# A complex MLP between two FFTs: one gelu over two PSUM banks, and eight PSUM banks split into four single and two double

## The chip, the core and the metric

The kernel runs on one core of a Trainium2 chip. A core has a matrix engine (TensorE, PE in the profile) that writes only to PSUM, three engines that read it or the on-chip memory SBUF (VectorE = DVE, ScalarE = ACT, GpSimd = POOL; POOL does not touch PSUM here), and queues for DMA. PSUM has eight banks; one bank holds 512 float32 values on each of 128 partitions. Each engine works through its own instructions in a fixed order and waits on semaphores for the others. The metric is device time in microseconds of one execution, lower is better.

## What is computed

The input is 8 images of 192 channels and 64 x 64 pixels, float32. Two layers follow each other. In short:

```python
# layer 0: attention in 8x8 windows over the 16 best keys, then an MLP
xs  = layernorm(x)                       # over channels
att = l2n(q) @ l2n(k).T * temperature
att = where(att >= kth_largest_16, att, -100) + rpb
x2  = xs + proj(softmax(att) @ v)
x2  = x2 + gelu(layernorm(x2) @ fc1) @ fc2
# layer 1: a small complex MLP between a 2D FFT and its inverse, then an MLP
freq = stack([real, imag](fft2(layernorm(x))))   # 2 values a frequency
h    = gelu(freq @ fc1.T + b1) @ fc2.T + b2      # 2 -> 16 -> 2, for each frequency
x    = x + ifft2(complex(h)).real
out  = x + gelu(layernorm(x) @ mlp1) @ mlp2
```

## The kernel before

One image at a time is held as `y` (channels on partitions). Layer 0 (`layer0`, `attention`, `mlp`) goes over 8 bands of 8 rows; each band has two halves of four attention windows. Layer 1 (`layer1`) first transposes the image so that rows lie on partitions (`px`, L411), then handles 24 blocks of 4 + 4 channels, transposes back (`pr`, L519) and ends with an MLP by bands.

One of the 24 blocks is a chain: normalization on POOL (L440, L444), a first DFT product `fa` (L454), copy on DVE (L462), a second DFT product `fz` (L464), copy (L466), then the pointwise complex MLP in two halves `hf`, then `fo` with its bias to SBUF (L491), and the inverse DFT products `fb` (L494) and `fy` (L508), each copied by DVE (L502, L511).

A half of the complex MLP has four first products `fh` (L472). They use 32 rows of the array each ("row tiles" k = 0..3) and each fills one bank. Four gelus on ACT (L481) bring these to SBUF, one bank each. Four second products (L482) each take one gelu output and use 32 columns of the array ("column tiles"); all write into the same bank `fo`, at 32 partitions each. The profile counts two matmul records for each float32 product, so a half has 8 records of L472 and 8 of L482.

All PSUM tiles come from one pool of eight one-bank buffers. A tile takes a free buffer and gives it back after its last reader. `fo` is held over both halves. The MLP (`mlp`, L196 to L214) holds two accumulators `mo` and takes a bank `mh` for each of six steps: first product L196, gelu L204 to the SBUF tag `h`, second product L206.

The parts of layer 0 and layer 1 are generators. While layer 0 of one image is issued, layer 1 of the image before is issued between its steps: 112 steps of layer 0 to 144 of layer 1, by a counter. A block of the FFT part has four such steps: normalization; `fa`, `fz` and the first half; the second half; `fo` to `fy`. The order within each engine follows this source order, except where an instruction's forerunners had not been placed yet when the engine's turn came; then a later one steps in. Layer 1 of the last image runs alone.

Of the kernel before, what the change touches and what calls it, by code (L numbers as in the profile page):

```python
# [8 lines left out]
FP = mybir.dt.float32  # L9
# [5 lines left out]
C = 192  # channels  # L15
HC = 96  # channels of one partition chunk
HW = 64  # rows, columns of an image; also tokens of one attention window
BAND = 512  # tokens of one band of 8 rows
# [6 lines left out]
def kernel(  # L25
# [6 lines left out]
    """Layer 0: layernorm, 8x8-window attention over the 16 best keys, projection, MLP.  # L32
    Layer 1: layernorm, FFT2, a pointwise complex MLP, inverse FFT2, MLP.

    One image at a time: `y` [96, 2, 4096] keeps its channels on partitions (channel
    c = 96 * chunk + partition) from layer 0's projection to the result. The FFTs are
    matrix products with 64-point DFT matrices, which take the data as the stationary
    operand where an axis has to change to the partitions.
    """
# [8 lines left out]
        tc.tile_pool(name="psp", bufs=8, space=bass.MemoryType.PSUM)  # L48
# [16 lines left out]
    vecs = load("vecs", [HC, 16])  # per-channel vectors, the two chunks of each side by side  # L65
    (g1, b1, g2, b2, fc2b, n2g, n2b, mlp2b) = (vecs[:, 2 * i : 2 * i + 2] for i in range(8))
    n1 = const.tile([128, 2, HC], FP, tag="n1", name="n1")  # on the partitions of each chunk
# [6 lines left out]
    # the biases of these two are a 193rd row, which the ones in row 96 of xn and ot multiply  # L74
# [8 lines left out]
    # relative position bias: partition (c, query), free (h3, key), head 3 c + h3. It is read  # L83
    # with the keys in reverse, where all of the table's strides are positive.
# [18 lines left out]
    # DFT matrices: two 64-point ones on the diagonal (fcos, fsin), and complex ones  # L103
    halves = load("halves", [128, 128])  # averages the two chunks' partitions
# [5 lines left out]
    # the pointwise complex MLP. Frequencies v lie on partitions as (v // 16, re/im, v % 16);  # L110
    # hidden values of 8 of them as (hidden 16, v % 8).
# [21 lines left out]
    # layer 0's normalized bands and heads' outputs, window by window, with a row of ones  # L133
# [8 lines left out]
    def windows(band):  # L142
        """A band's tokens [p, 512], as [p, row, window, column]."""
        return band.rearrange("p (r w k) -> p r w k", r=8, w=8)

    def layernorm(src, gam, bet, dst, nm, by_window=False):
        """src, dst [96, 2, 512]; by_window: dst's tokens are in the order of windows."""
# [42 lines left out]
    def mlp(hn, w1, bias1, w2, bias2, res, nm):  # L190
        """res [96, 2, 512] += gelu(hn @ w1 + bias1) @ w2 + bias2"""
        acc = [psum(f"mo_{nm}_{c}") for c in range(2)]
        for f in range(6):
# [9 lines left out]
            h = sb.tile([128, BAND], FP, tag="h", name=f"h_{nm}_{f}", bufs=5)  # L203
# [14 lines left out]
    # The parts below are generators: they yield between steps, so that one image's layer 1  # L218
    # can be issued between the steps of the next image's layer 0.

    def attention(xn, hb, nm):
        """Windows 4 hb .. 4 hb + 3 of a band: xn -> heads' outputs in ot."""
# [16 lines left out]
        # q and k by their norms, q by the temperature  # L239
# [32 lines left out]
        # scores: partition (c, query), free (h3, window, key)  # L272
# [18 lines left out]
        # where(s >= the 16th largest, s, -100) + rpb  # L291
# [22 lines left out]
        # softmax  # L314
# [14 lines left out]
        # keys to the partitions: (window of a pair, key), free (h3, pair, c, query)  # L329
# [23 lines left out]
        # a window's place is 4 hb + 2 p + w2  # L353
        ow = ot[:HC, :, 256 * hb : 256 * hb + 256].rearrange("q c (p w t) -> q w c p t", p=2, w=2)
        for w2 in range(2):
            nc.vector.tensor_copy(
                ow[:, w2], po[w2][:HC, :256].rearrange("q (c p t) -> q c p t", c=2, p=2)
            )

    def layer0(b, y):  # L360
        """x[b] -> y, by bands of 8 rows"""
        for i in range(NB):
            nm = f"{b}_{i}"
            yb = y[:, :, i * BAND : (i + 1) * BAND]
# [271 lines left out]
```

## Time and profile before

Three runs took 12977.23, 12985.01 and 12985.38 us, median 12985.01. All further numbers are of one profiled execution.

| | before |
|---|---|
| median of the runs | 12985.01 us |
| the profiled execution, span from first to last instruction | 12957.8 us (27.2 us under the median; nothing around it is listed) |
| PE busy | 8896.2 us, 69% |
| DVE / ACT / POOL busy | 3575.0 / 2861.4 / 1881.7 us |
| mean granted TensorE clock | 0.755 of full speed |
| complex MLP: first products, gelus, second products, busy | 820.7 / 945.1 / 1320.2 us |

In the profile, "L482 PE MATMUL fo<-fh,w2t x8" means eight records of the matmul on line 482, which write the tile `fo` from `fh` and `w2t`. A number in square brackets is the idle time of that engine just before, with the engine and line that ended it. Busy times of overlapping matmuls are modelled, so starts are firmer than ends. A granted clock of 0.5 means that the matrix engine got half of its clock pulses.

### The profile page before, as it was taken

How to read it: one execution, taken by the hardware profiler on the slowest of the kernel's cores; microseconds unless marked ns; L12 is line 12 of the kernel's file. 1: busy time of each engine (PE TensorE's matmuls, PEld its weight loads, DVE VectorE, ACT ScalarE, POOL GpSimd, SP SyncE). 2: the span in 40 equal slices, each digit the busy share in tenths (PEclk: the TensorE clock that was granted, in tenths of full speed). 3: DMA queues.
4: the chain of work that ended last, by engine and by line, in shares of the span. 5: the costliest groups of instructions: out<-in, count | busy, mean ns of one | idle time of the engine just before them, and what ended most of it. 6: DMA issues, size and time to landing. Idle time of an engine off the chain costs nothing.

```text
span 12957.8 us, 100088 instructions
## 1 busy us (share of the span) xinstructions
PE 8896.2 (69%) x38816; PEld 3927.9 (30%) x38816; DVE 3575.0 (28%) x12526; ACT 2861.4 (22%) x4820; POOL 1881.7 (15%) x1874
## 2 busy tenths in 40 slices
PE   4455776857768577685776766767667676767778
PEld 2222323323333233332333322333223332333323
DVE  2323223222232322323223222232222322232211
ACT  1111222212221222212222122221222212222121
POOL 1113011130011301103101131011211103011200
PEclk7666777867778677786777867778677776777898
DMA  0000000000000000000000000000000000000000
GB/s 17 3 4 3 3 2 3 10 4 3 3 3 9 4 3 3 3 11 2 3 3 3 11 2 3 3 4 10 3 2 3 5 9 3 2 3 3 8 1 10
DMA packets 28818, 60.28 MB, mean 5 GB/s; under 512 B 6834, under 2 KB 9331, under 8 KB 28340
## 3 DMA queue, kind: packets, MB, share of 16 engines
q1 hardware_dynamic: 21172, 28.70, 0.8%
q0 software_dynamic: 7168, 25.17, 0.7%
q8 instruction: 304, 4.98, 0.2%
q14 instruction: 174, 1.43, 0.0%
HBM read 28.69 MB, written 25.17 MB: 4 GB/s over the span
## 4 chain that ended last, share of the span: by engine, by line
PE 61%; DVE 18%; POOL 14%; ACT 5%; issue 2%; SPq 0%; DMA 0%; POOLq 0%; ACTq 0%; DVEq 0%
PE mo_l L206 12%; PE mh_l L196 12%; PE fo L482 8%; PE fh L472 5%; POOL nrm L251 4%; PE pq L233 3%; PE pp L380 2%; DVE s L298 2%; PE qt L264 2%; PE fy L508 2%; POOL xy L440 2%; PE fz L464 2%; PE fa L454 2%; PE fb L494 2%; POOL s L307 2%
## 5 line engine op out<-in xcount | busy, mean ns | idle before, releaser
L482 PE MATMUL fo<-fh,w2t 128*32 128x512 f32 x3072 | 1320.2, 791 | 254.6 <-ACT fh L481 254.6
L481 ACT ACTIVATE fh<-fh,ab 128x512 f32<-128x512 f32 x1536 | 945.1, 691 | 1738.1 <-PE fh L472 1732.1
L264 PE MATMUL qt<-ident,qk 128*96 128x128 f32 x1024 | 248.6, 424 | 1272.1 <-DVE qk L256 1272.1
L204 ACT ACTIVATE h_l<-mh_l,fcb 128x512 f32<-128x512 f32 x768 | 527.9, 687 | 2522.5 <-PE mh_l L196 2519.3
L472 PE MATMUL fh<-fz,w1t 32*128 32x512 f32 x3072 | 820.7, 879 | 205.6 <-DVE fz L466 205.6
L196 PE MATMUL mh_l<-hm,wmlp 96*128 96x512 f32 x1536 | 867.4, 694 | 30.1 <-ACT hm L182 30.1
L206 PE MATMUL mo_l<-h_l,wmlp 128*96 128x512 f32 x1536 | 846.3, 680 | 56.8 <-ACT h_l L204 56.8
L206 PE MATMUL mo_l<-h_l,wfc 128*96 128x512 f32 x1536 | 790.3, 639 | 57.3 <-ACT h_l L204 56.9
L196 PE MATMUL mh_l<-hn,wfc 96*128 96x512 f32 x1536 | 798.1, 643 | 9.8 <-ACT hn L182 9.8
L482 PEld LDWEIGHTS fo<-fh,w2t 128*32 128x32 f32 x3072 | 224.7, 121 | 1269.7 <-ACT fh L481 1117.6
L214 DVE SCALAR_TENSOR_TENSOR y<-mo_l,vecs,y 96x512 f32<-96x512 f32 x256 | 190.5, 746 | 1512.9 <-PE mo_l L206 1499.5
L264 PEld LDWEIGHTS qt<-ident,qk 128*96 128x96 f32 x1024 | 186.2, 196 | 1319.0 <-DVE qk L256 1311.3
L307 POOL TENSOR_TENSOR s<-s,rpb 128x768 f32<-128x768 f32 x128 | 231.1, 1805 | 2249.5 <-DVE mask L302 2087.6
L464 PE MATMUL fz<-fa,fwd 128*128 128x512 f32 x384 | 307.4, 893 | 364.0 <-DVE fa L462 364.0
L233 PE MATMUL pq<-wqkv,xn 96*128 96x384 f32 (+1 forms) x1024 | 527.4, 602 | 16.2 <-ACT xn L182 16.2
L251 POOL TENSOR_TENSOR nrm<-nrm,mhalf 128x24 f32<-128x24 f32 x128 | 536.9, 4194 | 10.1
L241 POOL TENSOR_TENSOR sq<-qk 128x768 f32<-128x768 f32 x128 | 187.8, 1467 | 2175.7 <-ACT qk L236 2175.7
L196 PEld LDWEIGHTS mh_l<-hm,wmlp 96*128 96x128 f32 x1536 | 338.8, 226 | 474.8 <-issue 407.4
L269 ACT COPY qkt<-qt 96x512 f32<-96x512 f32 x256 | 149.4, 584 | 1398.4 <-PE qt L264 1398.4
L491 DVE TENSOR_SCALAR fo<-fo,ab 128x512 f32<-128x512 f32 x192 | 143.4, 747 | 1109.7 <-PE fo L482 1109.7
L196 PEld LDWEIGHTS mh_l<-hn,wfc 96*128 96x128 f32 x1536 | 316.8, 210 | 433.7 <-issue 407.2
L334 PE MATMUL at<-ident,a 128*128 128x128 f32 x768 | 167.2, 366 | 392.6 <-DVE a L324 392.6
(120 smaller groups left out, 12085.9 us busy)
## 6 DMA issues: line engine op xcount, KB each, us to landing
xin<-in_x SPq DMA_DIRECT2D x64, 384.0 KB
out<-y POOLq DMA_DIRECT2D x64, 384.0 KB, 3.4
wfc<-in_wfc SPq DMA_DIRECT2D x2, 576.0 KB
wmlp<-in_wmlp SPq DMA_DIRECT2D x2, 576.0 KB
rrev<-in_rpb SPq DMA_DIRECT2D x48, 2.0 KB
wqkv<-in_wqkv SPq DMA_DIRECT2D x1, 218.2 KB
wqkv<-in_wqkv SPq DMA_DIRECT2D x1, 216.0 KB
n<-in_n SPq DMA_DIRECT2D x2, 48.0 KB
```

Of the source, the lines that this page charges most:

```text
L196: nc.tensor.matmul(ph, w1[:, c, f * 128 : (f + 1) * 128], hn[:, c, :], start=(c == 0), stop=(c == 1),)
L204: nc.scalar.activation(h, ph, AF.Gelu, bias=bias1[:, f : f + 1])
L206: nc.tensor.matmul(acc[c][:HC, :], w2[:, f, c * HC : (c + 1) * HC], h, start=(f == 0), stop=(f == 5),)
L233: nc.tensor.matmul(dst, tok, wqkv[:k, c, cols], start=(c == 0), stop=(c == 1))
L251: nc.gpsimd.tensor_tensor(nf, nf, mhalf[:, :24], ALU.pow)
L264: nc.tensor.transpose(pt[:HC, c * 256 + p * 128 : c * 256 + (p + 1) * 128], qk[:, p, j * C + c * HC : j * C + (c + 1) * HC], ident,)
L298: nc.vector.match_replace(s2[:, h3, wi], top[:, i, 0], s[:, h3, wi], -3.0e38)
L307: nc.gpsimd.tensor_tensor(s, s, rpb.unsqueeze(2).to_broadcast([128, 3, 4, 64]), ALU.add)
L464: nc.tensor.matmul(pz, fwd2, fa, start=True, stop=True)
L472: nc.tensor.matmul(phs[k], w1t[rows, hf].rearrange("p h v -> p (h v)"), fz[rows, :], start=True, stop=True,)
L481: nc.scalar.activation(h, phs[k], AF.Gelu, bias=ab[:, 0:1])
L482: nc.tensor.matmul(po[32 * k : 32 * k + 32, :], w2t[:, hf].rearrange("p a v -> p (a v)"), h, start=(hf == 0), stop=(hf == 1),)
```

## The change

The four one-bank tiles of a half become two tiles of two banks (`psum_wide`, from a pool of its own with two buffers). One gelu covers both banks of such a tile, 1024 columns. Its output `fh` has its own SBUF tag with three buffers of 1024 columns. The second products are issued in a loop of their own after both gelus. The one-bank pool shrinks from eight buffers to four, which now serve everything else. The tag `h` goes from five to three buffers (only the MLPs use it now), the tag `f` from four to three. Comments and docstrings are dropped; lines after the pool are some numbers further down in the new file.

```diff
     psp = ctx.enter_context(
-        tc.tile_pool(name="psp", bufs=8, space=bass.MemoryType.PSUM)
+        tc.tile_pool(name="psp", bufs=4, space=bass.MemoryType.PSUM)
+    )
+    psw = ctx.enter_context(
+        tc.tile_pool(name="psw", bufs=2, space=bass.MemoryType.PSUM)
     )
...
+    def psum_wide(name):
+
+        return psw.tile([128, 2, 512], FP, tag="pw", name=name)
...
-            h = sb.tile([128, BAND], FP, tag="h", name=f"h_{nm}_{f}", bufs=5)
+            h = sb.tile([128, BAND], FP, tag="h", name=f"h_{nm}_{f}", bufs=3)
...
-            f32 = lambda name: sb.tile([128, 512], FP, tag="f", name=f"{name}_{nm}", bufs=4)
+            f32 = lambda name: sb.tile([128, 512], FP, tag="f", name=f"{name}_{nm}", bufs=3)
...
             for hf in range(2):
-                phs = [psum(f"fh_{nm}_{hf}_{k}") for k in range(4)]
+
+                phs = [psum_wide(f"fh_{nm}_{hf}_{j}") for j in range(2)]
                 for k in range(4):
                     rows = slice(32 * k, 32 * k + 32)
                     nc.tensor.matmul(
-                        phs[k],
+                        phs[k // 2][:, k % 2],
                         w1t[rows, hf].rearrange("p h v -> p (h v)"),
                         fz[rows, :],
                         start=True,
                         stop=True,
                     )
+                hs = []
+                for j in range(2):
+                    h = sb.tile([128, 2, 512], FP, tag="fh", name=f"fh_{nm}_{hf}_{j}", bufs=3)
+                    nc.scalar.activation(h, phs[j], AF.Gelu, bias=ab[:, 0:1])
+                    hs.append(h)
                 for k in range(4):
-                    h = sb.tile([128, 512], FP, tag="h", name=f"fh_{nm}_{hf}_{k}", bufs=5)
-                    nc.scalar.activation(h, phs[k], AF.Gelu, bias=ab[:, 0:1])
                     nc.tensor.matmul(
                         po[32 * k : 32 * k + 32, :],
                         w2t[:, hf].rearrange("p a v -> p (a v)"),
-                        h,
+                        hs[k // 2][:, k % 2],
                         start=(hf == 0),
                         stop=(hf == 1),
                     )
```

## The prediction

> **What bounds the kernel now.** I read the page first, for which engine carries the chain that ended last and which groups of the complex MLP cost most.
>
> ```profile
> span 12957.8 us, 100088 instructions
> ...
> PE 61%; DVE 18%; POOL 14%; ACT 5%; issue 2%; SPq 0%; DMA 0%; POOLq 0%; ACTq 0%; DVEq 0%
> ...
> L482 PE MATMUL fo<-fh,w2t 128*32 128x512 f32 x3072 | 1320.2, 791 | 254.6 <-ACT fh L481 254.6
> L481 ACT ACTIVATE fh<-fh,ab 128x512 f32<-128x512 f32 x1536 | 945.1, 691 | 1738.1 <-PE fh L472 1732.1
> ...
> L472 PE MATMUL fh<-fz,w1t 32*128 32x512 f32 x3072 | 820.7, 879 | 205.6 <-DVE fz L466 205.6
> ```
>
> PE, in the order in which it was given its work, is the chain for 61% of the span; ACT as an engine is far from full, but its gelus stand inside PE's waits. So what counts is how long PE needs from the first `fh` of a block to its last `fo`. There are 192 blocks (8 images x 24), 384 halves.
>
> Then the timeline of the last image's FFT part, where nothing else runs: one half undisturbed.
>
> ```profile
> 12343.51 1.14 PE L472 MATMUL fh<-fz,w1t 32*128 32x512 f32 x8
> 12344.73 2.42 ACT L481 ACTIVATE fh<-fh,ab 128x512 f32<-128x512 f32 x4 [2.25 <-PE fh L472]
> ...
> 12345.47 2.78 PE L482 MATMUL fo<-fh,w2t 128*32 128x512 f32 x8 [0.82 <-ACT fh L481]
> ...
> 12348.29 0.75 DVE L491 TENSOR_SCALAR fo<-fo,ab 128x512 f32<-128x512 f32 x1 [9.50 <-PE fo L482]
> ```
>
> Four row-tiled products take 1.14 us together, then four gelus in 2.42 us set the pace, and the last second product ends 1.05 us after the last gelu. 4.74 us in all. The column-tiled products already overlap: each starts when its gelu is done, 0.58 us apart.
>
> Third, the timeline over all 192 blocks, for PE's order within each. Counted by that order there are six patterns: 38 blocks straight (first products, second products, twice), 42 with the scores `s` between the halves, 21 with a whole attention projection step, 21 with a whole layer-0 MLP between the halves, 35 with `at` transposes among the second products of the first half, and 35 of this kind (matmuls first, then ACT):
>
> ```profile
> 6292.75 2.09 PE L472 MATMUL fh<-fz,w1t 32*128 32x512 f32 x8 [2.35 <-DVE fz L466]
> 6295.60 1.91 PE L482 MATMUL fo<-fh,w2t 128*32 128x512 f32 x2 [0.76 <-ACT fh L481]
> 6297.45 2.08 PE L472 MATMUL fh<-fz,w1t 32*128 32x512 f32 x4
> 6299.76 1.91 PE L482 MATMUL fo<-fh,w2t 128*32 128x512 f32 x2 [0.23 <-ACT fh L481]
> 6301.60 2.07 PE L472 MATMUL fh<-fz,w1t 32*128 32x512 f32 x2
> 6303.60 1.92 PE L482 MATMUL fo<-fh,w2t 128*32 128x512 f32 x2
> 6305.45 2.07 PE L472 MATMUL fh<-fz,w1t 32*128 32x512 f32 x2
> 6307.45 3.62 PE L482 MATMUL fo<-fh,w2t 128*32 128x512 f32 x10
> ```
> ```profile
> 6294.86 0.69 ACT L481 ACTIVATE fh<-fh,ab 128x512 f32<-128x512 f32 x1 [11.46 <-PE fh L472]
> 6295.57 1.28 ACT L321 ACT_TABLE_LOAD   x1
> 6296.86 0.84 ACT L321 ACTIVATE a<-a 128x768 f32<-128x768 f32 x1
> ...
> 6299.02 3.00 ACT L481 ACTIVATE fh<-fh,ab 128x512 f32<-128x512 f32 x5
> ```
>
> The softmax's exp, with its table load and the one back to gelu, stands in ACT's order between the first gelu and the second. PE's order was made round it: one second product, then first products of the other half, one at a time. A row-tiled and a column-tiled product don't run together: each change costs about 2 us, as much as four of a kind side by side. These blocks take 18.35 us from the first `fh` to L491; a straight one with its clock at half (6.55 us a half, from 6226.09 to 6232.64) would take some 12.5 to 13.
>
> ```profile
> 6292.70:6311.10 18.40, 17.32 (x32) 3.06 (x32) 3.96 (x5) 8.47 (x11) 0.00 (x0) 0.50 0.00 0
> ```
>
> In this row of the view by windows (length, then PE, weight loads, DVE, ACT and POOL busy, then the granted clock) PE is busy for 17.32 us and yet has half its clock throughout.
>
> **The change, part by part.**
>
> *Wide gelus in order.* A copy on ACT of 256 columns takes 380 ns (L288), of 512 columns 584 ns (L269): 0.80 ns a column. So a second bank adds 0.41 us, and a wide gelu takes 0.69 + 0.41 = 1.10 us; a second one ends 0.58 + 0.41 = 0.99 later. Two wide gelus: 2.09 us against 2.42, a gain of 0.33 a half. The first second product waits 0.41 longer, which costs nothing, since the last gelu sets the end; the last two then run side by side in 1.05, as the overlapping pairs do now. Of 384 halves, 70 lie in the 35 blocks with exp, 42 second halves (after `s`) end behind DVE's search for the largest keys, where L491 waits anyway, and 21 second halves follow the MLP and are taken there. 251 x 0.33 = 83 us gain. Ends: 50 (more of them end in DVE or POOL waits) and 115 (all).
>
> *Blocks with exp.* After the first wide gelu two second products are free, not one, and of the other half only the first pair of first products finds a wide buffer. PE's order should be 4 fh, 2 fo, 2 fh, 2 fo, 2 fh, 4 fo. With half-clock rows: 2.09 + 0.02 + 1.10, then exp's 3.47 (from the end of a gelu to the next, 6295.55 to 6299.02), second gelu ends at 7.8; two second products to 9.7, two first ones to 11.8, last gelu to 12.9, two second ones to 14.9. Gain 18.35 - 14.95 = 3.4. If exp goes ahead of both or behind both, halves stay whole: 2.09 + 3.47 + 2.1 + 2.0 + 2.09 + 2.1 + 2.0, with the waits between 16.1, gain 2.2. Taken: between the two, 2.85 x 35 = 100 us. Ends: 0 (a new alternation as long as the old) and 6 x 35 = 210 (straight).
>
> *Four banks for all else, the layer-0 MLP.* I counted from the timeline, for each one-bank tile other than `fh`, how many other such tiles are live when its first product starts, and how long until only three are. 166 us of waiting in all, not overlapped. Its largest part is this place:
>
> ```profile
> 6176.81 1.96 PE L206 MATMUL mo_l<-h_l,wfc 128*96 128x512 f32 x4
> 6178.60 1.88 PE L196 MATMUL mh_l<-hn,wfc 96*128 96x512 f32 x4
> ...
> 6186.87 1.12 PE L472 MATMUL fh<-fz,w1t 32*128 32x512 f32 x2
> ```
>
> In 21 MLPs (three an image, seven images) `fo` is held from the first half to the second. With `fo` and two `mo` live, one bank is left for `mh`. Today PE starts the next `mh` before the gelu of the last is read; with one bank it waits: 84 times, 0.95 us each, 80 us. What is queued behind is everything PE does later. What covers it is the first products of the second half, which have buffers of their own and already slip in once (row 6186.87). If one slips into each of four gaps (1.05 each, one gap of 0.83 left) then the three products and four gelus that now follow the MLP (4.1 us to the end of `fo`, 6189.81 to 6193.97) shrink to 1.1: net cost 1 us an MLP, 20 in all. Taken 60, nearer to the counted row. Ends 20 and 88 (5 gaps x 0.83 x 21).
>
> *Four banks, elsewhere.* The rest of the count is 87 us: scores or `at` that start while a layer-1 MLP still holds two `mo` and an `mh` (46 us), transposes `px` beside `s` (10), layernorm tiles, `pr`. A part repeats the same wait for tiles queued behind each other, `px` is a filler. Taken 40; ends 10 and 87. Layer-1 MLPs never meet `fo`, so two `mh` remain, and PE is one `mh` ahead at most: nothing.
>
> *At nothing:* gelu outputs three deep and `h` three deep (PE is never more than two steps behind a gelu); `f` three deep (`fb` takes the place of `fa`, whose reader is two products back); copies of layer 0 behind a wide gelu wait up to 0.41 us more, beside PE's first products. No DMA moves.
>
> *Sum:* -83 - 100 + 60 + 40 = -83 us: span 12875. The profiled execution's 12957.8 is 27 under the median of 12985.0, so 12902.
>
> The Trainium skill ("TensorE: Matmul & The Clock Gate", Part 1) says that about 3.4 us of sustained activity bring the full clock; the row above, 17 us busy at half clock, disagrees, as if a quarter of the array did not count as activity. By the page the new order in these 35 blocks would run at full clock and end with ACT at some 10 us, an estimate of -290 for that term in place of -100.
>
> **The rivals.**
> *A, the alternation stays.* PE's order is laid down anew and exp may fall where first and second products still take turns. For it: the pattern comes from the order of placing, which durations shift. Against: only two turns are possible. Then -83 + 60 + 40 = +17: 13002.
> *B, slower: one bank too few.* PE takes everything in order, so a wait for a bank also delays what stands behind it, and that its own bank. If the 166 us of waits pass on a second time, the cost is 332, the sum +149, 13134; at 1.25 times, 13010. It decides from 183 us of cost. Against: `fh` leaves this pool, and more than four other tiles are live for only 148 us of the span.
> *C, the clock.* With longer gaps before `fo` more halves run at half clock: 6.55 against 4.74 us, 1.8 each. From 46 of 384 halves on, the gain is gone; at 80, 12902 + 144 = 13046. Against: the last image keeps 1.00 with gaps of 1.75 us.
> *D, better.* The 35 blocks go straight (-210) and fillers hide the bank waits (30 for both): -263, 12722.
>
> **How the numbers follow.** Forecast 0.46, its own range 12830 to 12960; A 0.18, B 0.14, C 0.06, D 0.16. To leave out 2 in 10, the range goes to 12740 (most of D) and to 13040 (A, and the smaller prices of B). 0.2% is 26 us, about what a measurement of this kernel can tell from none. Faster: forecast (0.44 of it) and D, 0.61 with a little of A; same: most of A's middle, 0.13; slower: the upper part of A, B, C, 0.26.
>
> **What would show it.** Gelus: 768 records of about 1.10 us; straight halves of 4.4 us. Blocks with exp: order 4-2-2-2-2-4 at about 15 us. MLPs with `fo` held: single `fh` records between `mh` and `mo`, or PE idle of 0.8 before `mo` on gelu L204. Wrong if PE's order shows other alternations, if `s` or `mh` wait for banks by more than 100 us, or if the granted clock falls below 0.73.

## The result, and the profile after

The changed kernel takes 13138.53 us (median of four runs, 13120.13 to 13151.71), the kernel before 12985.19 beside it: a ratio of 1.012, with a 95% interval from 1.0105 to 1.0134. It is slower, where 12902 was forecast with a range of 12740 to 13040. Its profiled execution has a span of 13118.4 us against 12957.8, and a mean granted clock of 0.746 against 0.755. The two spans lie 20 and 27 us under their medians; stages and blocks below are read from such single executions.

The page of the kernel after: span, the chain of waits by engine, and the groups of second products, gelus and first products (busy, mean of one in ns, then the idle time before them).

```profile
span 13118.4 us, 98779 instructions
...
PE 60%; DVE 18%; POOL 13%; ACT 6%; issue 2%; SPq 0%; DMA 0%; POOLq 0%; ACTq 0%; DVEq 0%
...
L493 PE MATMUL fo<-fh,w2t 128*32 128x512 f32 x3072 | 1069.3, 831 | 561.0 <-ACT fh L490 561.0
L490 ACT ACTIVATE fh<-fh,ab 128x1024 f32<-128x1024 f32 x768 | 817.1, 1113 | 1531.7 <-PE fh L480 1531.3
...
L480 PE MATMUL fh<-fz,w1t 32*128 32x512 f32 x3072 | 834.2, 862 | 203.5 <-DVE fz L473 203.5
```

The wide gelu costs what was worked out, 1.11 us, and ACT's busy time for these gelus falls by 128 us (945.1 to 817.1). But PE's wait in front of the second products more than doubles, from 254.6 to 561.0 us.

The timeline of the last image, where nothing else runs, one block. Each row has its start, its length, the engine and the operation.

```profile
12567.55 1.14 PE L480 MATMUL fh<-fz,w1t 32*128 32x512 f32 x8 [0.78 <-DVE fz L473]
12568.78 2.12 ACT L490 ACTIVATE fh<-fh,ab 128x1024 f32<-128x1024 f32 x2 [11.34 <-PE fh L480]
12569.95 1.05 PE L493 MATMUL fo<-fh,w2t 128*32 128x512 f32 x4 [1.26 <-ACT fh L490]
12570.93 1.12 PE L480 MATMUL fh<-fz,w1t 32*128 32x512 f32 x2
12571.98 1.85 PE L493 MATMUL fo<-fh,w2t 128*32 128x512 f32 x4
12573.76 1.98 PE L480 MATMUL fh<-fz,w1t 32*128 32x512 f32 x6
12575.83 2.12 ACT L490 ACTIVATE fh<-fh,ab 128x1024 f32<-128x1024 f32 x2 [4.93 <-PE fh L480]
12577.00 2.06 PE L493 MATMUL fo<-fh,w2t 128*32 128x512 f32 x8 [1.26 <-ACT fh L490]
```

Two records are one product here. PE waits 1.26 us for a wide gelu where it waited 0.82 for a narrow one. And a block that was straight (four first, four second products, twice) is now 4-2-1-2-3-4: one first product of the other half stands between the two pairs of second products. The next pair of second products takes 1.85 us where the first took 1.05: the clock has dropped in between.

The view by windows over 100 us of the last image (length, then busy time of PE, weight loads, DVE, ACT and POOL, the granted clock, the DMA share and GB/s), first the kernel before, then the kernel after:

```profile
12350.00:12450.00 100.00, 71.79 (x367) 26.21 (x365) 18.76 (x29) 29.07 (x48) 0.00 (x0) 1.00 0.00 1
```
```profile
12500.00:12600.00 100.00, 72.56 (x302) 25.64 (x302) 15.16 (x24) 21.20 (x20) 0.00 (x0) 0.83 0.00 0
```

PE is just as busy and finishes 302 matmul records in place of 367: its mean clock has fallen from 1.00 to 0.83.

A block with exp, matmuls and ACT in order of time:

```profile
6321.98 2.09 PE L480 MATMUL fh<-fz,w1t 32*128 32x512 f32 x8 [2.29 <-DVE fz L473]
...
6323.85 1.28 ACT L328 ACT_TABLE_LOAD   x1 [11.23 <-DVE a L325]
6325.15 0.84 ACT L328 ACTIVATE a<-a 128x768 f32<-128x768 f32 x1
...
6327.30 2.12 ACT L490 ACTIVATE fh<-fh,ab 128x1024 f32<-128x1024 f32 x2
6328.47 1.92 PE L493 MATMUL fo<-fh,w2t 128*32 128x512 f32 x4 [4.40 <-ACT fh L490]
6330.32 2.07 PE L480 MATMUL fh<-fz,w1t 32*128 32x512 f32 x2
6332.32 1.92 PE L493 MATMUL fo<-fh,w2t 128*32 128x512 f32 x4
6334.18 2.00 PE L480 MATMUL fh<-fz,w1t 32*128 32x512 f32 x6
```

The exp now stands ahead of both gelus, PE waits 4.40 us for it, the products on both sides of the wait run at half clock (2.09 and 1.92 us), and then first and second products still take turns, though fewer times than before.

Two tables show where the time went. The first cuts the profiled span at the first and last matmul of each stage: sums over images 0 to 6, and then the last image's FFT part.

| us | before | after | change |
|---|---|---|---|
| first image's layer 0 | 1057.5 | 1064.2 | +6.7 |
| FFT parts, images 0 to 6 | 6951.6 | 6947.2 | -4.4 |
| `pr`, images 0 to 6 | 794.4 | 808.2 | +13.8 |
| layer-1 MLPs, images 0 to 6 | 2232.5 | 2276.9 | +44.4 |
| last image's FFT part | 417.1 | 522.9 | +105.8 |
| all else | 1504.7 | 1499.0 | -5.7 |

The second gives the mean time of a block, from its first `fh` to the bias that takes its `fo`, by what stands among its products. It is taken from the timeline of each kernel. PE idle inside it is in brackets.

| blocks | number | before | after | sum of the change |
|---|---|---|---|---|
| exp | 35 | 18.39 (1.07) | 17.85 (5.65) | -19 |
| scores `s` | 42 | 13.06 (2.63) | 13.53 (3.36) | +20 |
| `at` transposes | 35 | 13.66 (0.76) | 14.58 (2.52) | +32 |
| layer-0 MLP | 21 | 34.16 (1.67) | 33.96 (1.26) | -4 |
| attention projection | 21 | 34.04 (18.01) | 30.91 (16.59) | -66 |
| others, images 0 to 6 | 14 | 9.47 (1.66) | 11.36 (3.08) | +26 |
| last image | 24 | 9.63 (1.67) | 12.44 (2.58) | +67 |

### The profile page after: what moved, and what is told of

It is laid out like the page before. It is cut to its first block, busy times and chain, and to the rows that moved or that the text cites. A ratio compares the mean times of both kernels' runs of the same rounds, so it can differ in the third digit from the quotient of the medians.

```text
span 13118.4 us, 98779 instructions
## 1 busy us (share of the span) xinstructions
PE 8786.7 (67%) x38816; PEld 3911.9 (30%) x38816; DVE 3592.8 (27%) x12526; ACT 2733.1 (21%) x4052; POOL 1876.2 (14%) x1874
## 4 chain that ended last, share of the span: by engine, by line
PE 60%; DVE 18%; POOL 13%; ACT 6%; issue 2%; SPq 0%; DMA 0%; POOLq 0%; ACTq 0%; DVEq 0%
PE mo_l L213 12%; PE mh_l L203 12%; PE fo L493 7%; PE fh L480 5%; POOL nrm L258 4%; PE pq L240 3%; ACT fh L490 3%; PE pp L387 2%; PE fy L519 2%; DVE s L305 2%; PE fa L461 2%; PE qt L271 2%; PE fb L505 2%; PE fz L471 2%; POOL xy L447 2%
## 5 line engine op out<-in xcount | busy, mean ns | idle before, releaser
L493 PE MATMUL fo<-fh,w2t 128*32 128x512 f32 x3072 | 1069.3, 831 | 561.0 <-ACT fh L490 561.0
L490 ACT ACTIVATE fh<-fh,ab 128x1024 f32<-128x1024 f32 x768 | 817.1, 1113 | 1531.7 <-PE fh L480 1531.3
L493 PEld LDWEIGHTS fo<-fh,w2t 128*32 128x32 f32 x3072 | 124.4, 123 | 1277.1 <-ACT fh L490 1066.5
L304 DVE MAX8 top<-s 128x8 f32<-128x64 f32 x1536 | 267.1, 210 | 641.6 <-ACT s L295 641.6
```

The costliest lines, as they stand in the source:

```text
L304: nc.vector.max(top[:, i, 0], s[:, h3, wi])
L490: nc.scalar.activation(h, phs[j], AF.Gelu, bias=ab[:, 0:1])
L493: nc.tensor.matmul(po[32 * k : 32 * k + 32, :], w2t[:, hf].rearrange("p a v -> p (a v)"), hs[k // 2][:, k % 2], start=(hf == 0), stop=(hf ...
```

## The experiments

Theories at the start: the loss is PE's order, laid down anew (O); the loss is PE's clock, which falls with longer gaps (C); the loss is the four banks left for everything else (B).

**Wide gelus, halves kept whole.** From the kernel after. The line only fixes the order in which PE gets its work: the first products of the second half come behind the last second product of the first half.

```diff
+                with tc.issue_after(last.ins) if hf else nullcontext():
                     for k in range(4):
...
-                    nc.tensor.matmul(
+                    last = nc.tensor.matmul(
                         po[32 * k : 32 * k + 32, :],
```

> The changed kernel with one thing more: the first products of a block's second half are placed on PE behind the last second product of the first half. In the last image the blocks then go 4-4-4-4 (first, second, first, second products) in place of 4-2-1-2-3-4. Theory T (the loss is PE's order: pairs of second products with a first product of the other half between them, and the clock that falls with it): the last image's FFT part, 523 us in the changed kernel and 418 before, goes to about 402 (24 x 2 x 0.33 under 418), its granted clock back to 0.95 or more, and the 35 interleaved blocks gain too: the whole at 12960 to 13020. Rival B (too few banks is the loss): the order does little, the whole stays over 13080. Rival C (the longer gap before the second products lowers the clock, whatever the order): the last image's clock stays near 0.74 and its FFT part over 500 us.

Measured: 12931.88 us, ratio 0.9965 (0.9952 to 0.9978). The exp blocks take 14.35 us, the last image's FFT part 423.7 us. A half of it, and a window:

```profile
12401.78 2.06 PE L494 MATMUL fo<-fh,w2t 128*32 128x512 f32 x8 [1.26 <-ACT fh L491]
...
12400.00:12500.00 100.00, 67.31 (x350) 25.00 (x342) 17.60 (x27) 25.43 (x24) 0.00 (x0) 0.91 0.00 0
```

One ordering line is worth 207 us. But even straight, the last image doesn't reach the 402 us that 48 gelu gains of 0.33 would give: its mean clock is 0.91.

**Narrow gelus, halves kept whole.** From the kernel before, with the same line.

```diff
+                with tc.issue_after(last.ins) if hf else nullcontext():
                     for k in range(4):
...
-                    nc.tensor.matmul(
+                    last = nc.tensor.matmul(
                         po[32 * k : 32 * k + 32, :],
```

> The kernel before (eight single banks, four narrow gelus) with the same one line of order. Only the 35 blocks with exp among their gelus change: 4-4-4-4 in place of 4-1-2-1-1-1-1-5. T: alternation was the cost of these blocks, 18.35 us becomes 12.5 (nothing but the half clock) to 16.1 (exp's 3.5 us on the path as well): 35 x 2.2 to 5.9 = 80 to 205 us less, 12780 to 12905. If alternation is not what these blocks cost (exp and the half clock are), they stay within 1 us and the whole within 30 us of 12985.

Measured: 12814.44 us, ratio 0.9873 (0.9857 to 0.989). The exp blocks fall from 18.39 to 15.07 us, the other classes move by less than 30 us each and the last image stays at 417.1. So the turns of first and second products had cost the kernel before some 116 us (35 x 3.32), and order without any wide gelu is better than the whole change with it.

**The split alone.** From the kernel before.

```diff
-        tc.tile_pool(name="psp", bufs=8, space=bass.MemoryType.PSUM)
+        tc.tile_pool(name="psp", bufs=4, space=bass.MemoryType.PSUM)
+    )
+    psf = ctx.enter_context(
+        tc.tile_pool(name="psf", bufs=4, space=bass.MemoryType.PSUM)
...
-                phs = [psum(f"fh_{nm}_{hf}_{k}") for k in range(4)]
+                phs = [
+                    psf.tile([128, 512], FP, tag="pf", name=f"fh_{nm}_{hf}_{k}") for k in range(4)
+                ]
```

> The kernel before with only the PSUM split: four single banks for the first products, four for all else, narrow gelus. T: the last image stays straight at 418 us; what the changed kernel loses outside the FFT part comes with the banks alone: the layer-1 MLP stretch 318 to 324 us an image, the transposes back 112 to 115, the first image's layer 0 +7, together about +73; the FFT part within 20 of before per image of all: 13030 to 13090. Rival B: the banks are the whole loss, 13110 or more. Rival C (gelu width is the whole loss): 12985 within 30.

Measured: 13240.99 us, ratio 1.0204 (1.0189 to 1.0219). So the split with narrow gelus is 102 us slower than the whole change. The exp blocks become longer, 21.42 us, since PE now takes turns one product at a time (4-1-1-1-1-1-1-1-1-4); that is 106 of the 256 us over the kernel before. The layer-1 MLPs take 2277.2 us, as in the kernel after. The blocks with an attention projection fall from 34.04 to 31.86 us, as in the kernel after, where they take 30.91: the first products of the second half now stand ahead of the `qt` transposes, which wait for DVE, and no longer behind them.

**One gelu over four banks.** From the kernel after: one tile of four banks, one gelu of 2048 columns.

```diff
-        tc.tile_pool(name="psw", bufs=2, space=bass.MemoryType.PSUM)
+        tc.tile_pool(name="psw", bufs=1, space=bass.MemoryType.PSUM)
...
-                for j in range(2):
-                    h = sb.tile([128, 2, 512], FP, tag="fh", name=f"fh_{nm}_{hf}_{j}", bufs=3)
-                    nc.scalar.activation(h, phs[j], AF.Gelu, bias=ab[:, 0:1])
-                    hs.append(h)
+                h4 = sb.tile([128, 4, 512], FP, tag="fh", name=f"fh_{nm}_{hf}", bufs=1)
+                nc.scalar.activation(h4, ph4, AF.Gelu, bias=ab[:, 0:1])
```

> The changed kernel with one four-bank tile and one gelu over 2048 columns a half in place of two of two banks. All four second products then become free at once, and PE's order is 4-4-4-4 by itself. T: straight halves of 1.14 + 0.08 + 0.69 + 3 x 0.42 + 0.05 + 1.1 = 4.3 us against 4.74 before, last image about 400 us, the 35 blocks without alternation; the bank cost outside the FFT stays (+73): 12860 to 12990 in all. Rival C: PE waits 2.1 us before the second products, so the clock falls in the last image and the whole goes to 13100 or more. Rival B: over 13080.

Measured: 13277.88 us, ratio 1.0232 (1.0216 to 1.0247). The halves are straight by themselves, the gelu takes 1.97 us in place of 2.42, and the last image's FFT part takes 534.2 us. Its second products and a window:

```profile
12610.92 1.93 PE L490 MATMUL fo<-fh,w2t 128*32 128x512 f32 x8 [2.13 <-ACT fh L488]
...
12600.00:12700.00 100.00, 67.56 (x278) 28.48 (x278) 15.29 (x24) 15.88 (x9) 0.00 (x0) 0.57 0.00 0
```

Nothing takes turns here, and still the mean clock is 0.57. So order isn't the only cause in the last image; the gap before the second products, 2.13 us here, is a candidate. In images 0 to 6 the blocks with `at` lose most, 20.23 us against 14.58 in the kernel after. The next four runs test order and gap each by itself in the last image.

**Order and gap, one at a time, in the last image.** All from the kernel before, with narrow gelus and eight banks; images 0 to 6 are left as they are. The first issues the last image's blocks as 4-2-1-2-3-4. The second and third issue its second products behind all four gelus of a half, from the last gelu backwards (3, 2, 1, 0, shown below) or with the second gelu first (1, 0, 3, 2), so that PE waits longer for the first of them.

```diff
+                phs = [first(0, k) for k in range(4)]
+                for k in range(2):
+                    second(0, k, gelu(0, k, phs[k]))
+                phn = [first(1, 0)]
+                for k in range(2, 4):
+                    second(0, k, gelu(0, k, phs[k]))
+                yield
+                phn += [first(1, k) for k in range(1, 4)]
```
```diff
+                    for k in (3, 2, 1, 0):
+                        nc.tensor.matmul(
+                            po[32 * k : 32 * k + 32, :],
```

> The kernel before (eight single banks, narrow gelus); only in the last image the source issues the blocks in the order that the changed kernel has there: 4-2-1-2-3-4. It separates the order from the width of the gelus. Last image's FFT part: 417 us before, 523 changed. If the order alone does it (two more turns of about 1 us a block, and then the clock): 465 with the clock at 0.95 or more, about 520 with the clock near 0.74. If the longer gap of the wide gelus is needed for the loss: 417 to 440. All else as before; the whole moves by the same amount.

> The kernel before; only in the last image the four second products of a half are issued as k = 3, 2, 1, 0, so that PE waits for the fourth gelu (2.5 us in place of 0.82) and then does all four together in 1.1. Same work, banks and turns; at full clock a half takes 4.8 us against 4.74, the last image's FFT part 420. If a longer gap lowers the clock by itself, as the kernel with the four-bank gelu (gap 2.13 us, granted clock 0.57 to 0.64) suggests: 510 to 550 and a clock of 0.55 to 0.7. If not: 417 to 425 at 0.95 or more.

> As the run with k = 3, 2, 1, 0, but in the order k = 1, 0, 3, 2: the gap before the second products is 1.40 us, near the 1.26 us of the two-bank gelu. If the clock depends on the gap: between, 420 to 445 for the last image's FFT part and a clock of 0.85 to 0.95, as in the changed kernel with the order held (424 us, 0.89 to 0.95). If the two-bank gelu's gap costs nothing: 417 to 420 at 0.99.

Measured: 12994.55, 13108.57 and 13018.12 us, ratios 1.0007 (0.9998 to 1.0017), 1.0094 (1.0079 to 1.0109) and 1.0022 (1.0013 to 1.0032). The last image's FFT part takes 428.5, 541.2 and 448.5 us, against 417.1. One window of each, in this order:

```profile
12400.00:12500.00 100.00, 77.49 (x358) 27.38 (x356) 18.06 (x28) 28.27 (x46) 0.00 (x0) 0.98 0.00 1
```
```profile
12400.00:12500.00 100.00, 63.09 (x276) 26.47 (x276) 14.39 (x22) 21.81 (x36) 0.00 (x0) 0.60 0.00 0
```
```profile
12400.00:12500.00 100.00, 67.86 (x322) 24.45 (x318) 16.75 (x26) 26.66 (x44) 0.00 (x0) 0.85 0.00 0
```

The turns alone cost 11 us and leave the clock at 0.98. The edit that makes the gap 1.3 to 1.4 us in place of 0.82 costs 31 us at a mean clock of 0.85, the one with 2.5 us costs 124 us at 0.60.

**The gap filled.** The run with the 2.5 us gap again, with two more products that nothing reads put into the gap of each half of the last image.

```diff
+                    dm = psum(f"dm_{nm}_{hf}")
+                    for _ in range(2):
+                        nc.tensor.matmul(dm, fwd2, fz, start=True, stop=True)
```

> As e6_last_gap_long (last image's second products in the order 3, 2, 1, 0, so that PE stands idle for 2.5 us in each half), with two more products of 128 x 128 by 512 columns, which nothing reads, issued into that gap in the last image alone. Two take 2.24 us with a full clock, so the gap shrinks to some 0.3. Theory 'PE's idle gap lowers the granted clock': the last image's FFT part goes back from 541 to 417 to 430 us although PE has 48 x 2.2 us more to do, the clock to 0.95 or more, and the time to within 0.3% of before (12985 to 13020). Rival 'it is the order 3, 2, 1, 0 or four overlapping second products at once': the clock stays at 0.6, and the two products make each half about 1.6 us longer: 610 or more, 13170.

Measured: 12967.85 us, ratio 0.999 (0.9981 to 1.0). The last image's FFT part goes from 541.2 to 411.3 us.

```profile
12416.22 1.98 PE L482 MATMUL dm<-fz,fwd 128*128 128x512 f32 x4
12418.78 1.06 PE L489 MATMUL fo<-fh,w2t 128*32 128x512 f32 x8 [0.58 <-ACT fh L486]
...
12400.00:12500.00 100.00, 73.81 (x411) 29.74 (x409) 19.41 (x30) 28.35 (x47) 0.00 (x0) 1.00 0.00 0
```

PE has 96 products more to do and needs 130 us less: the clock is back at 1.00. For the gap of 2.5 us this shows the cause, PE's idle time, and rules out the order of the second products. It is even 6 us under the kernel before, with its four second products of a half side by side in 1.06 us.

**The wide gelu's gap filled.** From the wide kernel with halves kept whole, one such product in each half of the last image.

```diff
+                if b == B - 1:
+                    dm = psum(f"dm_{nm}_{hf}")
+                    nc.tensor.matmul(dm, fwd2, fz, start=True, stop=True)
```

> As e1_wide_ordered (wide gelus, halves kept whole), and in the last image alone one more product of 128 x 128 by 512 columns, which nothing reads, between the first products and the second ones of each half: 1.12 us in a gap of 1.26. Theory 'the gap lowers the clock': the last image's FFT part falls from 424 to 402 us (417 of before less 48 x 0.33), with a clock of 0.97 or more, so 22 us under e1_wide_ordered (12932): 12910. Rival 'wide gelus gain nothing in a straight half': it stays at 417 or more with the clock restored; rival 'the clock falls for another reason': 424 or more with a clock of 0.91.

Measured: 12879.62 us, ratio 0.9925 (0.991 to 0.9939). The last image's FFT part falls from 423.7 to 409.9 us, with this window:

```profile
12400.00:12500.00 100.00, 78.63 (x387) 29.67 (x380) 19.50 (x30) 23.40 (x23) 0.00 (x0) 0.94 0.00 0
```

14 of the expected 22 us: the wide gelu then gains 7 us of its 16 against the kernel before, and the mean clock stays at 0.94 with PE busier than before. The total fell by 52 us, more than the last image explains. The rest lies in images 0 to 6, which the edit leaves alone (see the next run).

The trace tells where the clock falls. In all sixteen kernels the recorded clock is either 1.00 or 0.50 and, between the first change and the last, it changes only on a grid of 3.41 us; a mean of 0.85 is a share of such windows. Seven of them in a row, from the run with the gap of 1.3 to 1.4 us:

```profile
12399.87:12403.29 3.42, 1.98 (x12) 0.29 (x8) 0.00 (x0) 2.42 (x4) 0.00 (x0) 1.00 0.00 0
12403.29:12406.70 3.41, 1.77 (x13) 1.13 (x10) 1.44 (x2) 0.00 (x0) 0.00 (x0) 1.00 0.00 0
12406.70:12410.11 3.41, 3.41 (x20) 2.47 (x20) 0.42 (x1) 0.00 (x0) 0.00 (x0) 0.50 0.02 5
12410.11:12413.53 3.42, 1.84 (x10) 0.61 (x10) 1.38 (x2) 0.00 (x0) 0.00 (x0) 1.00 0.00 0
12413.53:12416.94 3.41, 2.09 (x12) 0.19 (x4) 0.00 (x0) 2.26 (x4) 0.00 (x0) 0.50 0.00 0
12416.94:12420.35 3.41, 3.41 (x16) 0.70 (x12) 0.00 (x0) 0.16 (x1) 0.00 (x0) 0.50 0.00 0
12420.35:12423.77 3.42, 1.97 (x12) 0.29 (x8) 0.00 (x0) 2.42 (x4) 0.00 (x0) 1.00 0.00 0
```

After the windows in which PE was busy for 1.77 and 1.84 us the clock falls, after the one with 1.98 it holds; at half clock it comes back after a busy 3.41, not after 2.09. Over the last images of the kernel before and of the seven runs whose windows are shown above, each of 100 falls came after a window at most 0.54 busy, and each of 104 returns after one at least 0.84 busy; full-clock windows between 0.51 and 0.54 went either way.

The fourth busy time, ACT's, tells what the windows before a fall held. With the gap of 2.5 us, all 16 full-clock windows with gelu work in them were followed by half clock (at most 0.31 busy). With the gap of 1.3 to 1.4 us none of 50 was: all its 21 falls came after windows of the DFT products, which the edit leaves as they are. So did 13 of the 14 falls of the straight wide kernel and all 9 with its gap filled. The kernel before has the same DFT products and only 2 falls. Its blocks take 17.05 us at full clock, nearly five windows (17.07), so the grid cuts one block like the next; the shortest blocks of the others take 16.95 and 16.50 us. That the grid then falls on the DFT products in a worse place would explain the 31 us, the 0.91 and the 0.94, but no run tests it.

**The SBUF tags alone.** From the kernel before: `h` three deep for the MLPs, a tag of its own, five deep, for the outputs of the narrow gelus, `f` three deep.

```diff
-            h = sb.tile([128, BAND], FP, tag="h", name=f"h_{nm}_{f}", bufs=5)
+            h = sb.tile([128, BAND], FP, tag="h", name=f"h_{nm}_{f}", bufs=3)
...
-            f32 = lambda name: sb.tile([128, 512], FP, tag="f", name=f"{name}_{nm}", bufs=4)
+            f32 = lambda name: sb.tile([128, 512], FP, tag="f", name=f"{name}_{nm}", bufs=3)
...
-                    h = sb.tile([128, 512], FP, tag="h", name=f"fh_{nm}_{hf}_{k}", bufs=5)
+                    h = sb.tile([128, 512], FP, tag="fh", name=f"fh_{nm}_{hf}_{k}", bufs=5)
```

> The kernel before with only the SBUF tags of the change: three h buffers for the MLPs alone, an fh tag of its own (five narrow buffers), three f buffers. Eight single banks, narrow gelus. The prediction put these at nothing: within 0.2% of before. A loss of 50 us or more would mean that the shallower tags make PE wait.

Measured: 13021.78 us, ratio 1.0029 (1.0019 to 1.0039). PE's order is that of the kernel before, and its idle time up to the last image's first DFT product is 3890.2 us against 3890.4, so no wait was added. What grew is PE's busy time in images 0 to 6, with a mean clock of 0.746 against 0.755 over the whole execution. The medians differ by 37 us, and in the run before this one some 38 us lay in images 0 to 6. (The three runs that edit the last image alone have FFT parts of 6970.9 to 6981.4 us there, against 6951.6; but the profiled execution of the kernel before lies 27 us under its median.) So some 40 us of a total can come from clock in places that no edit touched; what brings it is open, and what follows is read from stages and blocks, not from totals alone.

**Split and order.** The narrow kernel with halves kept whole, and the banks split into 4 and 4 as in the run of the split alone.

```diff
-        tc.tile_pool(name="psp", bufs=8, space=bass.MemoryType.PSUM)
+        tc.tile_pool(name="psp", bufs=4, space=bass.MemoryType.PSUM)
+    )
+    psf = ctx.enter_context(
+        tc.tile_pool(name="psf", bufs=4, space=bass.MemoryType.PSUM)
```

> The narrow gelus of before, first products of the second half issued behind the second products of the first (as in e2_narrow_ordered), and the PSUM banks split into 4 for fh and 4 for all else. Nothing but the split differs from e2_narrow_ordered (12814.4 us). Theory 'the four banks cost what the split kernels show outside the blocks': layer-1 MLPs +44, pr +14, first layer 0 +7, and inside the FFT part the attention and MLP blocks of the wide ordered kernel against the narrow ordered one (1.6 us in 42 blocks with s, 1.0 in 35 with at, 0.5 in 21 with an MLP, gained back 3.9 in 21 with qkv: +30), together e2 + 95: 12910, ratio to before 0.994, and wide gelus are worth about -20 net of the clock. Rival 'the wide gelu itself, and not the split, slows the FFT part of the wide ordered kernel': only the 65 us outside it, 12880 or less, ratio 0.992 or less.

Measured: 12849.18 us, ratio 0.9897 (0.9882 to 0.9912); its profiled execution lies 28 us under that. The rival holds: with the order fixed the split costs little, 35 us over the narrow kernel with halves kept whole, which is within what two builds can differ by through the clock. The layer-1 MLPs (+44.5) and `pr` (+21.7) lose, the projection blocks gain (35.37 to 31.66 us, 78 in all). The wide gelus, with the second products behind both and with the SBUF tags of the change, are then what separates 12849 from 12932: their blocks with `s` take 14.24 us against 12.70, with `at` 14.92 against 13.72, and the largest gain is 0.69 us in each of the exp blocks (14.35 against 15.04). In the blocks with `at` PE's idle time is 2.51 us against 0.76. How much of the 83 us each of the three brings wasn't tested.

**Banks for layer 1.** As the last, but layer 1 takes banks from the four of `fh`, which stand empty outside its FFT part: first `px`, `pr` and the MLP with its layernorm, then the MLP with its layernorm alone, then `pr` alone. The diff is that of the first; the others leave out the lines of the rest.

```diff
+    def psum_f(name):
+        return psf.tile([128, 512], FP, tag="pf", name=name)
...
-            ph = psum(f"mh_{nm}_{f}")
+            ph = psum_h(f"mh_{nm}_{f}")
...
-            px = psum(f"px_{b}_{q}")
+            px = psum_f(f"px_{b}_{q}")
...
-            pr = psum(f"pr_{b}_{q}")
+            pr = psum_f(f"pr_{b}_{q}")
...
-            layernorm(yb, n2g, n2b, hn, f"d{nm}")
+            layernorm(yb, n2g, n2b, hn, f"d{nm}", psum=psum_f)
...
-            mlp(hn, wmlp1, fcb[:, 1, :], wmlp2, mlp2b, yb, f"l1_{nm}")
+            mlp(hn, wmlp1, fcb[:, 1, :], wmlp2, mlp2b, yb, f"l1_{nm}", psum_h=psum_f)
```

> As e9_split_ordered (narrow gelus, order held, banks 4 and 4), but layer 1 outside its FFT part takes its banks from the four that hold fh, which stand empty there: px, pr, the layernorm of the layer-1 MLP and its mh. Theory 'the layer-1 MLP, pr and px pay for having four banks': the layer-1 MLPs of images 0 to 6 go back from 2277 to about 2232 us, pr from 817 to 795, px from 1016 to 1007, the FFT part stays at 6737: 75 us under e9_split_ordered (12849), 12774, ratio to before 0.984, and under e2_narrow_ordered (0.987). Rival 'the split costs there through the clock, or through another order, not through banks': these stretches stay as they are in e9_split_ordered, 12849.

Measured: 12246.45 us, ratio 0.9434 (0.9418 to 0.945), the fastest kernel of all. Eight times the expected gain, so neither theory holds. PE's order in the FFT part is unchanged (6723.3 us); outside it, it is new. The two runs that take it apart:

> As e9_split_ordered, with the four banks of fh given to the layernorm and the mh of the layer-1 MLP alone; px and pr stay in the other four, with PE's order as in e9_split_ordered up to the end of pr. Theory 'the layer-1 MLPs hold up layer 0 of the next image, since its tiles queue behind theirs for four banks': most of the 603 us comes from here, as PE gets other work into the gaps between mh and mo: 12849 - 450 = 12400, with pr still at 110 us or more an image. Rival 'only the wait for a bank goes': the MLPs fall from 2277 to 2232 us, 12804. Rival 'it is pr': 12849 to 12830.

> As e9_split_ordered, with the four banks of fh given to pr alone; the layer-1 MLP as in e9_split_ordered. Theory 'the layer-1 MLPs are the place': pr falls from 817 to some 200 us in seven images, but its place in layer 0's steps is taken by the layer-1 MLP that now starts sooner only in part, 12849 - 100 = 12750. Rival 'it is pr, which by its sixteen pieces in turn with layer 0's steps holds up the MLP': 12849 - 500 = 12350.

Measured: 12427.33 us, ratio 0.9568 (0.9554 to 0.9582), for the MLP alone, and 12780.24, ratio 0.9837 (0.9821 to 0.9853), for `pr` alone. So the layer-1 MLPs are the place: seven of them take 1937.2 us in place of 2277.0. (With banks for `pr` alone, `pr` falls from 817 to 196 us, but the stretch of the MLPs grows by 598, as PE then does there the layer-0 work that had stood among `pr`.) One of them as a window, first with the four shared banks (the kernel with split and order), then with its own:

```profile
7016.00:7328.00 312.00, 261.76 (x747) 107.54 (x748) 61.07 (x184) 60.92 (x91) 24.58 (x29) 0.85 0.03 9
```
```profile
6854.00:7117.00 263.00, 236.45 (x747) 98.47 (x746) 60.39 (x186) 60.51 (x91) 23.63 (x29) 0.94 0.04 11
```

The same 747 products. PE's idle time falls by 24 us, and its busy time by 25, since its clock rises from 0.85 to 0.94. The end of a band in the timeline, in the same two kernels:

```profile
7069.11 1.02 PE L199 MATMUL mh_l<-hm,wmlp 96*128 96x512 f32 x2
7070.98 1.96 PE L209 MATMUL mo_l<-h_l,wmlp 128*96 128x512 f32 x4 [0.62 <-ACT h_l L207]
7073.85 0.30 PE L161 MATMUL lt_d<-ident,y 96*128 96x96 f32 x1
...
7075.84 0.65 PE L161 MATMUL lt_d<-ident,y 96*128 96x96 f32 x4 [0.70 <-DVE st_d L167]
7079.29 1.06 PE L179 MATMUL lc_d<-ident,xh_d 128*96 128x128 f32 x4 [2.80 <-DVE xh_d L173]
```
```profile
6900.88 1.02 PE L202 MATMUL mh_l<-hm,wmlp 96*128 96x512 f32 x2
...
6902.18 0.50 PE L164 MATMUL lt_d<-ident,y 96*128 96x96 f32 x4
6902.74 1.96 PE L212 MATMUL mo_l<-h_l,wmlp 128*96 128x512 f32 x4
...
6909.42 1.20 PE L182 MATMUL lc_d<-ident,xh_d 128*96 128x128 f32 x6 [0.43 <-DVE xh_d L176]
```

With a rotation of its own the next band's layernorm starts ahead of the last `mo` and fills PE's wait for the last gelu; with one rotation for all it comes behind. In this MLP PE waits 1.2 us for `st_d` in place of 8.3, and 1.1 for `h_l` in place of 7.9. The two runs bring 422 and 69 of the 603 us of the first; where the rest comes from, `px` or the two together, wasn't taken apart.

## Why the prediction was wrong, point by point

*Wide gelus in order, -83.* The step that failed is "the first second product waits 0.41 longer, which costs nothing, since the last gelu sets the end". The gelu's size was right (1.11 us for 1.10), and so was the wait, 1.26 for 0.82. At full clock the halves are shorter, too: straightened, the last image's shortest blocks take 16.50 us for 17.05. But the term has no clock in it. Straightened, the last image has 20 of 123 windows at half clock against 6 of 121 before, and takes 424 us where 402 would have been right. That PE's idle time can lower the clock is shown at 2.5 us, by the filled gap; at 1.3 to 1.4 us a like edit cost 31 us, by falls that follow the DFT products. In the kernel after the blocks lost in four of the classes: +20, +32 and +26 us in images 0 to 6 and +106 in the last image's FFT part. Not all of it is clock: in the blocks with `at` the mean clock is 0.83 before and 0.84 after, in the "others" 1.00 in both, and there PE idles 1.8 and 1.4 us longer. How this splits into turns, waits and neighbours' order wasn't tested.

*Straight halves stay straight.* This was taken for granted and stands in no term. In the 38 straight blocks first and second products now take turns: 4-2-1-2-3-4 in the last image, and with a next band's layernorm between the last second products in the other 14. Turns alone cost 11 us in the last image, the edit to the gap alone some 31; together, in the kernel after, the last image loses 106 and what the gelus should bring. The two are worth more together than apart: straightened, the wide kernel needs 424 us there, 99 less. In the kernel after, the 38 falls of the clock there are of two kinds: 19 after windows of the DFT products, and 19 after windows with gelus, nearly all of them 0.63 to 0.66 busy, which in no other kernel's last image brought a fall; why the turns lower that bound is open. That turns between the two kinds cost time agrees with the Trainium skill ("TensorEngine Tiling (Array Packing)", Tiling Modes, Key Properties), by which a change of the tiling mode drains PE.

*Blocks with exp, -100, measured -19.* The step that failed is "PE's order should be 4 fh, 2 fo, 2 fh, 2 fo, 2 fh, 4 fo", with exp between the gelus. Exp went ahead of both and, against "halves stay whole" for that case, the halves did not: 4-2-1-2-3-4 again. With the order held the same blocks take 14.35 us, 141 us less than before and between the two prices for whole halves (77 at 2.2 each, 210 at 6), so what failed was the order and not the size. The low end, 0, "a new alternation as long as the old", was the nearest.

*Layer-0 MLP with `fo` held, +60, measured -4.* The mechanism came as described: single first products between `mh` and `mo`, four in each MLP. Its price was too high, as those products covered all of the waits: PE idles 1.26 us in such a block, against 1.67.

*Four banks elsewhere, +40.* By stages +44 in the layer-1 MLPs, +14 in `pr`, +7 in the first image, and -66 in the projection blocks, where first products now fill the wait for `qt`. The failed step is "layer-1 MLPs never meet `fo` ... nothing": they are where the split costs most, 6.3 us an image, and the count of live tiles missed it. The last runs show that even eight shared banks cost there: it is the shared rotation, not the number, as a rotation of four of its own, for the layernorm and `mh`, is faster by 42 us an image than the eight shared ones were (277 against 319).

*SBUF tags at nothing.* No wait and no change of order came from them; the 37 us of that run lie in the clock.

*The rivals.* A (turns stay) was right about the order, but not about the sum. B (banks) ended near the measured time, 13134, by luck: its mechanism, waits for banks that pass on, isn't what the runs show. The split alone does cost 256 us, of which 106 are turns in the exp blocks and 45 the layer-1 MLPs; the rest wasn't taken apart. With the order held it costs 35. C (the clock) named a part of the cause, at 0.06. Its price of 1.8 us a half can't be checked alone: the last image loses 2.2 a half, but some 38 of its 106 us lie outside the blocks' complex MLP, and turns share in it. Its "against" was a misreading: "the last image keeps 1.00 with gaps of 1.75 us". No gap between PE's products there is longer than 0.84 us in the kernel before. And it was the full clock of one pattern of work, close to where it falls: some windows there are 0.52 busy.

*The page on the clock.* The Trainium skill ("TensorE: Matmul & The Clock Gate", Part 1) has the clock fall after an idle window of about 3.4 us. The windows of this trace are as long, 3.41 us, but they need not be idle: the clock fell after windows in which PE was busy for up to 0.54 of the time, and with turns up to 0.66. The same part also tells of a kernel whose short idle times between groups of products made the clock swing. In the last image of the kernel after, where no gap is longer than 1.54 us, it swings likewise, with 38 falls in 523 us.

## What to carry to other kernels

Where one engine's order carries the chain and its clock follows its activity, don't call a longer wait free because something later sets the end: look for stretches of 3.4 us in which the engine would be busy for about half or less, as idle time there costs clock as well as time. A mean busy share doesn't show them, and a full clock before the change may be close to the bound. Before merging instructions, look at what the larger piece does to the first wait and to the order laid down around it; one line that held the order was worth more here (-171 us on the kernel before) than the merged gelus. Tiles that share one rotation can hold each other up in order, so give stages that overlap in time banks of their own: that, with the order held, took 5.7% off the kernel before.

## What the runs showed of the hardware that was not expected

- The granted clock is 1.00 or 0.50 and changes on a grid of 3.41 us. In the last images of eight kernels it fell only after windows in which PE was busy for at most 0.54, and came back only after windows of at least 0.84; in the kernel after, with its turns, also after 0.63 to 0.66. Idle gaps of 2.5 us in each half kept it at a mean of 0.60; products that nothing reads, put into the gap, brought 541 us down to 411.
- The mean clock isn't a function of the mean busy share: 78.6% busy ran at 0.94 (wide, gap filled) and 71.8% at 1.00 (before). The falls of the first all came after windows of the DFT products, 0.52 to 0.54 busy.
- Two kernels with the same order and the same idle time on PE differ by 37 us of 13000 through the clock in the interleaved part. Repeated runs of one build spread over up to 36 us, so a small difference between two builds needs a look at its stage before it is given a cause.
